# Block sums of the step-0 weights made from the first half step on, and copies of the original blocks issued by SyncE at later half steps

## The chip, the core and the metric

The kernel runs on one core of one Trainium2 chip. The metric is the device time of one execution in microseconds (us). A core has five engines that run side by side and meet at semaphores: TensorE (PE, matmul), VectorE (DVE), ScalarE (ACT), GpSimd (POOL) and SyncE (SP). Here SyncE and ScalarE issue the DMAs. Every engine takes its own instructions in program order, so an instruction that waits holds up all that stand behind it on the same engine.

## The reference

Two blocks follow each other on x (2 batches, 2048 rows, 512 features), all in float32:

```
mod = t @ Wm + bm                         # shifts, scales, gates from the condition
y   = y + gate_a * s5(ln(y) * (1 + scale_a) + shift_a)      # a linear recurrence over time
y_mod = (ln(y) * (1 + scale_c) + shift_c) * (1 + scale_ff) + shift_ff
y   = y + gate_ff * (gelu(y_mod @ W1 + b1) @ W2 + b2)       # 512 -> 2048 -> 512
h   = gamma * (ln(y) * ln_g + ln_b) + beta                  # gamma, beta from the condition
q, k, v = h @ Wqkv.T + bqkv               # 16 heads of 32
out = (softmax(q k^T) / sqrt(512)) v @ Wp.T + bp
h1  = out + y;  result = sln(h1) + h1
```

Only the first block and the q, k, v products matter for this change.

## The kernel before

The rows are cut into 8 chunks of 512. Up to about 1150 us the program goes through steps 0 to 7: step i does the feed-forward of chunk i beside the recurrence of chunk i + 1 and the q, k, v products of chunk i - 1. Attention follows.

**Seven products for eight.** From step 1 on, every product with w1, w2, wk, wq and wv is a two by two block product done with seven block products. For that each weight matrix is needed as seven blocks: three of its four original blocks (index 0, 3 and 4) and four sums or differences of blocks (1, 2, 5 and 6). They are made once, in step 0, and stored in DRAM: `w1d` (8 parts), `wkd` (2 parts for k, 2 for q), `wvd` (2 parts) and `w2d` (8 parts). From step 1 on `more` (line 866) streams them back through a ring of four tiles, `wring`. Its first three slots are those of the plain weights wk, wq and wv.

**Step 0 itself** (lines 1064 to 1076) still uses the plain weights. It runs over f = 0 to 15. For each f, `ff_first` (line 593) multiplies by one column block of w1 and ScalarE applies gelu to give `hid` (line 600); `ff_second` (line 604) multiplies by w2 for f - 1. After `ff_first` and after `ff_second` the program calls `run_due`, so there are 32 half steps, numbered h = 2f or 2f + 1; what the dictionary `due` lists for a half step is written into the program there, in order of the list. The order is fixed by hand.

What `due` held already (lines 1030 to 1048 and 1054 to 1058): `gate_of_feed_forward` at h = 2 and `rest_of_mod` at h = 3, both through `modulate` (line 235); `s5_gates` at 4; at 5 `rows_of_biases`, the norm of chunk 1 (`normalised`), its turn into features (`s5_blocks`: four VectorE transposes, line 498, then 16 DMAs on SyncE, line 503) and `s5_direct` (12 GpSimd operations); `s5_features` (ScalarE, line 479) at 10 to 13; `s5_in` (TensorE, line 531) and `s5_turn` (lines 541 and 543) at 13; `s5_scan` and a load of x at 14; `s5_out` (lines 578 to 582) at 18 to 21; at 22 three `more` on SyncE, then `ff_norm` and `by_blocks` (again transposes and 16 DMAs, this time `moved`); `ff_features` (ScalarE, line 479) from 26.

`modulate` lets TensorE make a product `pq`, ScalarE copy it to the tile `quarters` (line 251), and TensorE sum the quarters (line 240). The tile's slot is `hid0`, `hid1` or `hid2` by m modulo 3: GATE_F (m = 5) and GAMMA (m = 8) use `hid2`, BETA `hid0`. These slots have one buffer.

**The jobs.** There are 22: jobs 0 to 7 for w1 (`by_columns`), 8 and 9 for wk, 10 and 11 for wq, 12 and 13 for wv (`by_rows_v`), 14 to 21 for w2 (`by_rows_w2`). Job n runs on VectorE if n mod 3 is 2, otherwise on GpSimd. `combine` (line 795) makes two pairs of sums with two operations each (lines 801, 802 and 805, 806) and issues a SyncE DMA of 256 KB for each pair (line 807). The first pair's tile is in slot `hi` (two buffers) for GpSimd or `hid2` (one buffer) for VectorE; the second pair's is in `lo` (two buffers, both engines). For w1, wk, wq and wv the job also issues three copies of original blocks, 128 KB each, through `plain` (line 810), on ScalarE's queue. `w2_originals` (line 852) does so for w2 with three copies of 1 MB. The weights themselves come in by SyncE loads ahead of step 0; wk, wq and wv are the last (line 767).

Of the kernel before, what the change touches and what calls it, by code (L numbers as in the profile page):

```python
# [39 lines left out]
def tile_s5_block_then_sln_attention(  # L40
# [21 lines left out]
    nc = tc.nc  # L62
# [49 lines left out]
    HC = CH // 2  # L112
    w1d = dpool.tile([FH, P, 7, HC], F32, name="w1d")
    w2d = dpool.tile([7, P, FH, HC], F32, name="w2d")
# [167 lines left out]
    w2_sb = [hpool.tile([P, FH, D], F32, name=f"w2_{j}", tag=f"h{j}") for j in range(2)]  # L282
# [147 lines left out]
    def norm_steps(b, c):  # L430

        held = {}

        def row(t):
            if t == 0:
                held["mv"] = small.tile([P, TT, 2], F32, name="ln_mv", tag=f"ln_mv{TT}")
            ln_row(xt[b, c], t, held["mv"])

        def scale():
            held["mean"] = small.tile([P, TT], F32, name="mean")  # L440
            held["rstd"] = small.tile([P, TT], F32, name="rstd")
            ln_scale(held["mv"], TT, held["mean"], held["rstd"])

        def to(t):
            if t == 0:
                xns[b, c] = xnp.tile([P, TT, D], F32, name="xn", tag="xn")
            normalise(xns[b, c][:, t, :], xt[b, c][:, t, :], held["mean"], held["rstd"], t)

        return [(row, t) for t in range(TT)], [(scale,)], [(to, t) for t in range(TT)]
# [69 lines left out]
    def tag_of(b, c):  # L519
        return f"f{index[b, c] % 2}"  # L520
# [72 lines left out]
    def ff_first(b, c, f):  # L593
        ph = ps1.tile([P, CH], F32, name="ph")
        for k in range(KC):
            nc.tensor.matmul(
                ph, w1_sb[:, k, f * P : (f + 1) * P], fts[b, c][:, k, :], start=k == 0, stop=k == KC - 1
            )
        hids[f] = work1.tile([P, CH], F32, name="hid", tag=f"hid{f % 2}", bufs=1)
        nc.scalar.activation(  # L600
            in_time(hids[f], b, c), as_made(ph, b, c), AF.Gelu_apprx_tanh, bias=vec[:, V_B1 + f : V_B1 + f + 1], scale=1.0
        )

    def ff_second(b, c, f):
        if f == 0:
            pos[b, c] = ps1.tile([P, TT, D], F32, name="po", bufs=1)
        hid = hids.pop(f)
        for t in range(TT):
            nc.tensor.matmul(
                pos[b, c][:, t, :], hid[:, t * P : (t + 1) * P], w2_sb[f // FH][:, f % FH, :],  # L610
                start=f == 0, stop=f == FC - 1,
            )
# [182 lines left out]
    def combine(block, to, *shape, engine=nc.gpsimd):  # L795

        for at, tag in ((1, "hi"), (5, "lo")) if engine is nc.gpsimd else ((1, "hid2"), (5, "lo")):
            pair = work1.tile([P, 2, HC], F32, name="sums", tag=tag, bufs=1 if tag == "hid2" else 2)
            views = [pair[:, m, :].rearrange("p (k f) -> p k f", k=shape[0]) for m in range(2)]
            if at == 1:  # L800
                engine.tensor_tensor(views[1], block(1, 0), block(1, 1), ALU.add)
                engine.tensor_tensor(views[0], views[1], block(0, 0), ALU.subtract)
                s2 = views[0]
            else:
                engine.tensor_tensor(views[0], block(0, 0), block(1, 0), ALU.subtract)
                engine.tensor_tensor(views[1], block(0, 1), s2, ALU.subtract)
            nc.sync.dma_start(to(at, at + 2), pair)

    def plain(block, to, m, i, j):
        nc.scalar.dma_start(to(m, m + 1), block(i, j))  # L810

    ORIGINALS = ((0, 0, 0), (3, 0, 1), (4, 1, 1))

    def by_columns(w, half, p, dst, engine):

        def block(i, j):
            return w[:, 2 * j : 2 * j + 2, half * i + P * p : half * i + P * p + P]

        def to(m0, m1):
            if m1 - m0 == 1:  # L820
                return dst[:, m0, :].rearrange("p (k f) -> p k f", k=2)
            return dst[:, m0:m1, :]

        combine(block, to, 2, engine=engine)
        for m, i, j in ORIGINALS:
            plain(block, to, m, i, j)

    def by_rows_w2(q, engine):

# [8 lines left out]
    def by_rows_v(w, q, engine):  # L838

        def block(i, j):  # L840
            return w[:, 2 * j + q : 2 * j + q + 1, HC * i : HC * i + HC]

        def to(m0, m1):
            return wvd[:, m0:m1, q, :]

        combine(block, to, 1, engine=engine)
        for m, i, j in ORIGINALS:
            plain(block, to, m, i, j)

    def w2_originals():  # L850
        for m, i, j in ORIGINALS:
            nc.scalar.dma_start(w2d[m], w2_sb[j][:, :, HC * i : HC * i + HC])

    stream, slots, ready = [], ["wk", "wq", "wv", "w3"], []
    for i in range(1, len(order)):
# [10 lines left out]
    def more(engine=nc.scalar):  # L866

        n = begun[0]
        if n == total:
            return  # L870
        begun[0] += 1
        tag = slots[n % 4]
        src, size = stream[n]
        w = (strip if tag == "w3" else wlate).tile([P, FH * HC], F32, name="wring", tag=tag)
        engine.dma_start(w[:, :size], src)
        ready.append(w)
# [21 lines left out]
    def ff_sums(b, c, engine):  # L898
        parts_of["ff"] = sums_of(*quarters_of(fts[b, c], TT), engine, TT, "parts")
# [121 lines left out]
    for i, now in enumerate(order[:1]):  # L1021

        due = {(f, h): [] for f in range(FC + 1) for h in range(2)}
        ahead = order[i + 1]

        def quarters_from(f, what, chunk):
            for k in range(KC):
                due[f + k // 2, k % 2].append((what, *chunk, k))

        due[1, 0].append((gate_of_feed_forward,))  # L1030
        due[1, 1].append((rest_of_mod,))
        due[2, 0].append((s5_gates, start[0]))
        due[2, 1].append((rows_of_biases,))
        due[2, 1].append((normalised, *ahead))
        due[2, 1].append((s5_blocks, *ahead))
        due[2, 1].append((s5_direct, *ahead))
        quarters_from(5, s5_features, ahead)
        due[6, 1].append((s5_in, *ahead))
        due[6, 1].append((s5_turn, *ahead))
        due[7, 0].append((s5_scan, *ahead))  # L1040
        quarters_from(9, s5_out, ahead)
        due[11, 0].append((ff_norm, *ahead))
        due[11, 0].append((by_blocks, *ahead, tag_of(*ahead)))
        quarters_from(13, ff_features, ahead)
        due[7, 0].append((load_x, *order[i + 2]))
        jobs = [(by_columns, w1_sb, FH * P, p, w1d[p]) for p in range(FH)]
        jobs += [(by_columns, w, HC, p, wkd[2 * n + p]) for n, w in enumerate((wk, wq)) for p in range(2)]
        jobs += [(by_rows_v, wv, q) for q in range(2)]
        jobs += [(by_rows_w2, q) for q in range(FH)]
        for n, job in enumerate(jobs):  # L1050
            h = 6 + 4 * n // 5
            due[h // 2, h % 2].append((*job, nc.vector if n % 3 == 2 else nc.gpsimd))
        due[9, 0].append((w2_originals,))
        for n in range(3):
            due[11, 0].insert(0, (more, nc.sync))

        later[order[2]] = norm_steps(*order[2])
        due[12, 1] += later[order[2]][0]

        def run_due(at):  # L1060
            for what, *args in due[at]:
                what(*args)

        for f in range(FC):
            ff_first(*now, f)
            run_due((f, 0))
            if f == FC - 1:
                first.close()
                strip = early.enter_context(tc.tile_pool(name="strip", bufs=1, side="right"))
                ff_sums(*ahead, nc.vector)  # L1070
                more()
            if f:
                ff_second(*now, f - 1)
            run_due((f, 1))
        ff_second(*now, FC - 1)
        ff_out(*now)
        first_banks.close()
        psq = early.enter_context(tc.tile_pool(name="psq", bufs=6, space=PSUM, side="right"))

    for i, now in enumerate(order):  # L1080
# [20 lines left out]
        if ahead:  # L1101
            rows, scale, to = later.pop(ahead)
# [57 lines left out]
        if ahead:  # L1160
            rows, scale, to = norm_steps(*ahead)
# [528 lines left out]
    keeps, m = [], 0  # L1690
# [16 lines left out]
    due = {}  # L1707
# [21 lines left out]
    for b in range(NB):  # L1729
        for c in range(NQ):  # L1730
            j = NP * (blocks.index((b, NPAIR - 1, c)) + 1) + 1
            if (b, c) == (LB, LC):
                most, rest = slice(0, NH - 4), slice(NH - 4, NH - 2)
                j = NP * (N - 1)
# [55 lines left out]
    def block_at(j):  # L1790
        n, i = divmod(j, NP)
        return (n, i) if 0 <= n < N else (None, i)

    for j in range(FIRST, NP * N + 2):
# [16 lines left out]
        n, i = block_at(j + AHEAD)  # L1811
# [26 lines left out]
        n, i = block_at(j + 1)  # L1838
# [4 lines left out]
        n, i = block_at(j - 1)  # L1843
# [59 lines left out]
```

## Time and profile before

| what | value |
|---|---|
| time, median of 3 runs | 3296.51 us (3296.01 to 3299.68) |
| time of the profiled execution | 3303.55 us |
| its span, first to last instruction | 3300.4 us |
| mean granted TensorE clock | 0.988 |
| step 0 on TensorE | 66.5 to 218.3 us |
| TensorE busy, 120 to 140 us | 15.57 of 20 us, clock 0.83 |
| TensorE busy, 200 to 220 us | 14.91 of 20 us, clock 0.91 |
| TensorE busy, 140 to 200 us | 60.0 of 60 us |

A line of the trace's order of time gives the start in us, the duration in us, the engine, the line of the kernel, the operation, the tile written and the tiles read, the shape, how many instructions were merged, and in brackets how long the engine was idle before and what ended that. An engine name with a q (SPq, ACTq) is its sequencer issuing DMAs; this is not counted as busy time. In a group line of the page the last part is the same idle time for the whole group.

### The profile page before, as it was taken

Reading aid. Unit: us, or ns where it says so; the run is one execution under the profiler, and the core shown is the slowest. Engines: PE = TensorE matmul, PEld = TensorE weight load, DVE = VectorE, ACT = ScalarE, POOL = GpSimd, SP = SyncE. Lnnn points to the kernel's source line nnn. Section 1 sums busy time; section 2 is a strip of 40 time slices with the busy share of each in tenths; the row PEclk is TensorE's granted clock in tenths of the full one; section 3 lists DMA queues with packets and bytes.
Section 4 is the critical chain, followed back from the end, with each engine's and each line's share of the span. In section 5 each row is a group of like instructions: output and inputs, shape, how many; then the busy total and the mean of one; then the engine's idle time right before and its main releaser. Section 6 shows DMA issues by size and latency. Waiting matters only on the chain.

```text
span 3300.4 us, 38742 instructions
## 1 busy us (share of the span) xinstructions
PE 3178.3 (96%) x12900; PEld 1768.0 (54%) x12900; DVE 2406.2 (73%) x3226; ACT 2015.7 (61%) x2393; POOL 2385.6 (72%) x1438
## 2 busy tenths in 40 slices
PE   7999999999999998999999999999999999999996
PEld 4458888888888884344444444444444444443432
DVE  5455565656565434888888888888888888888884
ACT  2111213121221212899999999999888898898862
POOL 1646454554546331799989999998899899999986
PEclk9999999999999998999999999999999999999998
DMA  8556757667575664332322223133233333333233
GB/s 306 186 173 185 234 177 229 196 195 246 157 241 174 221 205 151 80 87 50 76 70 56 70 65 74 50 78 80 70 80 92 85 77 93 79 75 87 66 102 97
DMA packets 298012, 422.18 MB, mean 128 GB/s; under 512 B 98712, under 2 KB 195224, under 8 KB 286678
## 3 DMA queue, kind: packets, MB, share of 16 engines
q1 hardware_dynamic: 254758, 269.63, 30.2%
q10 hardware_dynamic: 43056, 150.09, 14.0%
q8 instruction: 102, 1.67, 0.2%
q14 instruction: 96, 0.79, 0.1%
HBM read 309.38 MB, written 87.94 MB: 120 GB/s over the span
## 4 chain that ended last, share of the span: by engine, by line
PE 25%; ACT 16%; DVE 13%; issue 3%; DMA 3%; POOL 1%; SPq 1%; ACTq 0%; DVEq 0%; POOLq 0%
PE o L1399 11%; PE s L1330 8%; DVE run L1346 7%; ACT x L1341 7%; ACT x L1389 5%; ACT pT L1389 4%; PE py L1482 3%; DVE pT L1384 3%; DVE run L1350 2%; PE pt_run L1358 1%; DMA by<-invd 1%; POOL x L1378 1%; PE pk L657 1%; DMA ks<-kd 1%; DVE st L1499 0%
## 5 line engine op out<-in xcount | busy, mean ns | idle before, releaser
L1378 POOL TENSOR_TENSOR x<-x,shift 128x1024 f32<-128x1024 f32 x704 | 1653.2, 2389 | 132.2 <-DMA shift<-flat 113.7
L1330 PE MATMUL s<-qs,ks 128*128 128x512 f32 x2688 | 823.1, 427 | 51.8 <-DVE run L1346 32.3
L1341 ACT COPY x<-s 128x1024 f32<-128x1024 f32 x704 | 691.8, 1010 | 148.6 <-PE s L1330 132.1
L1346 DVE TENSOR_TENSOR run<-s,run 128x1024 f32<-128x1024 f32 x576 | 705.1, 1224 | 80.7 <-ACT x L1341 36.8
L1389 ACT ACTIVATE x<-x 128x1024 f32<-128x1024 f32 x704 | 738.0, 1058 | 20.6 <-POOL x L1378 20.0
L1399 PE MATMUL o<-x,v 128*64 128x512 f32 x2816 | 718.1, 612 | 0.0
L1330 PEld LDWEIGHTS s<-qs,ks 128*128 128x128 f32 x2688 | 444.7, 189 | 466.1 <-DVE run L1346 161.0
L1384 DVE TENSOR_TENSOR pT<-s,shift 128x1024 f32<-128x1024 f32 x320 | 388.8, 1215 | 50.5 <-PE s L1330 50.5
L1350 DVE TENSOR_TENSOR run<-s,run 128x1024 f32<-128x1024 f32 x320 | 389.2, 1216 | 10.1 <-PE s L1330 9.7
L1389 ACT ACTIVATE pT<-pT 128x1024 f32<-128x1024 f32 x320 | 339.4, 1061 | 74.7 <-DVE pT L1384 74.6
L1399 PE MATMUL o<-pT,v 128*64 128x512 f32 x1280 | 329.2, 593 | 6.6 <-ACT pT L1389 6.6
L1399 PEld LDWEIGHTS o<-x,v 128*64 128x64 f32 x2816 | 157.1, 135 | 309.5 <-issue 251.3
L920 PE MATMUL pp<-parts,wring 128*128 128x256 f32 x1344 | 318.0, 379 | 0.0
L973 PE MATMUL pp<-wring,h 128*128 128x256 f32 x1344 | 293.3, 379 | 0.0
L973 PEld LDWEIGHTS pp<-wring,h 128*128 128x128 f32 x1344 | 255.4, 190 | 39.8 <-issue 5.7
L920 PEld LDWEIGHTS pp<-parts,wring 128*128 128x128 f32 x1344 | 255.9, 190 | 35.0
L920 PE MATMUL pp<-fT,wring 128*128 128x256 f32 x1008 | 249.5, 381 | 7.6 <-ACT hid L619 2.8
L920 PEld LDWEIGHTS pp<-fT,wring 128*128 128x128 f32 x1008 | 191.1, 190 | 39.2 <-DVE zb L957 3.8
L1399 PEld LDWEIGHTS o<-pT,v 128*64 128x64 f32 x1280 | 91.3, 137 | 191.3 <-issue 142.3
L1096 POOL TENSOR_TENSOR h<-h 128x256 f32<-128x256 f32 x56 | 42.7, 763 | 191.1 <-ACT h L1094 191.1
L1346 DVE TENSOR_TENSOR run<-s,x 128x1024 f32<-128x1024 f32 x64 | 78.4, 1225 | 114.2 <-ACT x L1341 114.2
L479 ACT ACTIVATE fT<-moved,s_shift,s_scale 128x512 f32<-128x512 f32 x28 | 20.5, 802 | 200.2 <-DMA moved<-fT 170.5
(379 smaller groups left out, 3111.6 us busy)
## 6 DMA issues: line engine op xcount, KB each, us to landing
wring<-w2d ACTq DMA_DIRECT2D x49, 1024.0 KB
wring<-w1d ACTq DMA_DIRECT2D x53, 896.0 KB
ks<-kd SPq DMA_DIRECT2D x128, 256.0 KB
shift<-flat SPq DMA_DIRECT2D x64, 512.0 KB
qs<-qd SPq DMA_DIRECT2D x496, 64.0 KB
wring<-wkd ACTq DMA_DIRECT2D x28, 896.0 KB
moved<-fT SPq DMA_DIRECT2D x168, 64.0 KB
x<-in_x SPq DMA_DIRECT2D x8, 1024.0 KB
```

Of the source, the lines that this page charges most:

```text
L920: nc.tensor.matmul(to, w[:, m, k, :], moving, start=start and k == 0, stop=stop and k == 1, skip_group_check=True,)
L973: nc.tensor.matmul(out[:, t * HC : t * HC + HC], x(m, q, t), w[:, q, :], start=start and q == 0 and t == 0, stop=stop and q == depth - 1 a ...
L1096: nc.gpsimd.tensor_tensor(h1[:, p, HC:], h1[:, p, HC:], h1[:, p, :HC], ALU.subtract)
L1330: nc.tensor.matmul(s[:, e, :], kst[pair_of[n], e][:, kt * P : (kt + 1) * P], qst[n][:, e, :], start=True, stop=True,)
L1341: nc.scalar.copy(x, s)
L1346: nc.vector.tensor_tensor(runs[n], s, kept[n, 0] if kt == 1 else runs[n], ALU.max)
L1350: nc.vector.tensor_tensor(runs[n], raw_scores(n, kt), runs[n], ALU.max)
L1378: nc.gpsimd.tensor_tensor(x, x, shifts[n], ALU.add)
L1384: nc.vector.tensor_tensor(x, s, shifts[n], ALU.add)
L1389: nc.scalar.activation(x, x, AF.Exp)
L1399: nc.tensor.matmul(outs[n][64 * e : 64 * e + 64, :], v[:, kt, e : e + 2, :], x[:, e, :], start=first, stop=final,)
L1482: nc.tensor.matmul(py, o4[:, g, :], wp[:, g, :], start=g == 0, stop=g == NG - 1)
```

## The change

The sums and the copies of originals become separate entries of `due`. A job called with an engine only makes sums and stores them; the same job called with `None` only copies the originals. The copies go from ScalarE's queue to SyncE's.

Jobs 0 to 13 (w1, wk, wq, wv) make their sums at half steps 0 to 4, at the front of each half step's list (of several at one half step the later job stands first); before, they were at 6 to 16, at the end of the lists. Jobs 14 to 21 (w2) make theirs at 6 to 13 instead of 17 to 22. The copies of jobs 0 to 13 are at 5 to 10, at the end of the lists, and those of w2 at 12 instead of 18.

```diff
     def plain(block, to, m, i, j):
-        nc.scalar.dma_start(to(m, m + 1), block(i, j))
+        nc.sync.dma_start(to(m, m + 1), block(i, j))
...
-        combine(block, to, 2, engine=engine)
-        for m, i, j in ORIGINALS:
-            plain(block, to, m, i, j)
+        if engine is None:
+            for m, i, j in ORIGINALS:
+                plain(block, to, m, i, j)
+        else:
+            combine(block, to, 2, engine=engine)
...
     def w2_originals():
         for m, i, j in ORIGINALS:
-            nc.scalar.dma_start(w2d[m], w2_sb[j][:, :, HC * i : HC * i + HC])
+            nc.sync.dma_start(w2d[m], w2_sb[j][:, :, HC * i : HC * i + HC])
...
         for n, job in enumerate(jobs):
-            h = 6 + 4 * n // 5
-            due[h // 2, h % 2].append((*job, nc.vector if n % 3 == 2 else nc.gpsimd))
-        due[9, 0].append((w2_originals,))
+            h = 5 * n // 14 if n < 14 else n - 8
+            engine = nc.vector if n % 3 == 2 else nc.gpsimd
+            due[h // 2, h % 2].insert(0, (*job, engine))
+        for n, job in enumerate(jobs[:14]):
+            h = 5 + 3 * n // 7
+            due[h // 2, h % 2].append((*job, None))
+        due[6, 0].append((w2_originals,))
```

`by_rows_v` changes as `by_columns` does.

More of the change, by code (lines that the diff above doesn't have):

```diff
@@ L844, in to @@
             return wvd[:, m0:m1, q, :]
-        combine(block, to, 1, engine=engine)
-        for m, i, j in ORIGINALS:
-            plain(block, to, m, i, j)
+        if engine is None:
+            for m, i, j in ORIGINALS:
+                plain(block, to, m, i, j)
+        else:
+            combine(block, to, 1, engine=engine)
     def w2_originals():
         for m, i, j in ORIGINALS:
-            nc.scalar.dma_start(w2d[m], w2_sb[j][:, :, HC * i : HC * i + HC])
+            nc.sync.dma_start(w2d[m], w2_sb[j][:, :, HC * i : HC * i + HC])
     stream, slots, ready = [], ["wk", "wq", "wv", "w3"], []
```

## The prediction

> **What bounds the kernel now.** I read the page first, for the shares; then the tensor engine's order of time through step 0, for its gaps; then the order of time of ScalarE, VectorE, GpSimd and SyncE around each gap. The page has TensorE busy for 96% of the span, and in its forty slices only the first falls well below the rest:
>
> ```profile
> PE 3178.3 (96%) x12900; PEld 1768.0 (54%) x12900; DVE 2406.2 (73%) x3226; ACT 2015.7 (61%) x2393; POOL 2385.6 (72%) x1438
> PE   7999999999999998999999999999999999999996
> ```
>
> So an edit inside step 0 (66 to 218 us) counts only through gaps of TensorE that it closes or opens; what it closes there is kept, since from 224 us on TensorE goes from matmul to matmul (20.0 us busy in most 20 us windows up to 420). Step 0 has two places that this edit can reach. TensorE's order of time (start, duration, idle before it):
>
> ```profile
> 125.94 1.88 PE L531 MATMUL pu<-fT,bT_re 128*128 128x512 f32 x4
> 130.17 1.13 PE L531 MATMUL pu<-fT,bT_re 128*128 128x512 f32 x2 [2.35 <-ACT fT L479]
> 133.37 2.07 PE L531 MATMUL pu<-fT,bT_re 128*128 128x512 f32 x2 [2.07 <-ACT fT L479]
> 135.24 5.34 PE L531 MATMUL pu<-fT,bT_im 128*128 128x512 f32 x8
> 140.42 3.60 PE L596 MATMUL ph<-fT,w_sb 128*128 128x512 f32 x8
> ...
> 202.48 3.60 PE L596 MATMUL ph<-fT,w_sb 128*128 128x512 f32 x8
> 209.50 8.83 PE L609 MATMUL po<-w,hid 128*128 128x512 f32 x16 [3.42 <-ACT hid L600]
> ```
>
> Eight full-speed matmuls take 3.43 us from start to start (140.42 to 143.85). **Place a**: the 16 of s5_in take 14.48 us (125.94 to 140.42) where 6.87 would do: 7.6 us lost. Both gaps wait for ScalarE's features, and between 132.0 and 138.8 the granted clock was 0.50. **Place b**: 3.59 us of wait, and 8.83 where 7.03 is usual (the clock was 0.51 from 210.5 to 213.9): 5.4 us lost.
>
> Why a? ScalarE's order of time; ACTq lines are DMAs that it issues:
>
> ```profile
> 118.71 6.00 ACTq L810 DMA_DIRECT2D w1d<-w_sb  x5
> 124.76 0.81 ACT L479 ACTIVATE fT<-fT,mod,u_scale 128x512 f32<-128x512 f32 x1 [7.47 <-DMA w1d<-w_sb]
> 126.99 1.65 ACTq L810 DMA_DIRECT2D w1d<-w_sb  x3
> ...
> 129.47 2.98 ACTq L810 DMA_DIRECT2D wkd<-wk  x3
> 132.51 0.81 ACT L479 ACTIVATE fT<-fT,mod,u_scale 128x512 f32<-128x512 f32 x1 [2.39 <-DMA wkd<-wk]
> ```
>
> The features' inputs had landed at 112.6 (the trace's landing records). ScalarE was held by copies it had to issue. A copy starts only once the eighth DMA before it in the program has landed: those issued at 118.71, 120.80, 122.67 and 123.80 follow landings at 118.69, 120.78, 122.64 and 123.77, mostly of sums that SyncE had issued after waiting for GpSimd. Why b? ScalarE waits 14.23 us for `moved` (207.36), which follows VectorE's second norm; that is late because gate products of s5_out wait behind block sums (L805 at 166.63 waited 5.25 us for a DMA, so pa of 158.4 is read at 167.31).
>
> **What is removed.** All 45 copies leave ScalarE. In order: hid 5, two features, hid 6, two features, each 0.7 to 0.8 us, so all four are done before TensorE needs them: **a, -7.6 us**. The block sums of w2 end by half step 13, before s5_out at 18. Then gate product, add, statistics, norm (3.82, still beside GpSimd's adds), turn (2.48) and 16 moves (194.62 to 207.10, 12.5 us) follow the last s5_out by some 25 us, and TensorE's work up to that place takes 31 us (175.02 to 206.08): **b, -5.4 us**. Cover there is 6 us; without it b returns.
>
> **What is added early.** The jobs of half steps 0 to 4 stand ahead of everything else there. The one to fear is slot hid2 (one buffer): VectorE's jobs 2, 5, 8, 11 use it, and so do the `quarters` that ScalarE writes in modulate for GATE_F (m = 5) and GAMMA (m = 8). In the new program GATE_F's quarters stand behind job 8 and must wait until its first pair of sums has landed in DRAM. The same reuse shows before:
>
> ```profile
> 98.43 1.22 DVE L801 TENSOR_TENSOR sums<-w_sb 128x256 f32<-128x256 f32 x1
> 99.68 1.37 DVE L802 TENSOR_TENSOR sums<-sums,w_sb 128x256 f32<-128x256 f32 x1
> 117.34 0.97 DVE L805 TENSOR_TENSOR sums<-w_sb 128x256 f32<-128x256 f32 x1 [16.29 <-POOL sums L805]
> ...
> 120.86 0.99 DVE L801 TENSOR_TENSOR sums<-w_sb 128x256 f32<-128x256 f32 x1 [1.69 <-issue]
> ```
>
> The pair made at 98 to 101 was issued only at 118.46 (SyncE had two GpSimd jobs before it), landed at 120.78, and the next VectorE job wrote hid2 at 120.86. The second half (L805) waited likewise for slot `lo`, which has two buffers for both engines.
>
> The chain in the new kernel, with these prices: two GpSimd sums 1.45 us (0.72 each), an issue 0.35, issue to landing 2.03 (113.83 to 115.87), 0.68 between landings. wv lands at 70.84 on the same queue, so job 2's pairs land at 71.5 and 72.2, job 1's at 72.9 and 73.6. GpSimd then fills `lo` for job 0 (73.7, landed 75.9), job 4's `lo` (77.4), job 3's hi (78.9) and `lo` (80.4). Job 5's first pair lands at 76.5, so VectorE makes job 8's by 78, but SyncE issues it behind job 3's, at 80.8: landed near 83.2. Quarters to 83.9, and the sums of L240 start at 84 to 85 where they started at 77.30: 7.2 us later. TensorE is idle for 4 to 6 us before, so the clock halves: the cases above and the 0.50 from 60.3 to 70.5 cost 1.5 to 3.4 us each, say 2.3. **Early: +9.5 us.** Bounds: 4.8, if the pairs needn't queue behind the loads (3.3 earlier, clock 1.5), to 11.4. GAMMA's quarters want job 11's pair, landed near 90; TensorE gets there at 93, so this hides. GpSimd's first sums (56.4 to 61) run beside VectorE's first norm and cost it about 1.6 us (L125, 0.17 alone, took 0.65 beside GpSimd at 185.44); the 84 us is reached anyway, so that is free here. SyncE issues the 28 early pairs by 107, and the turn of the next chunk, slowed by GpSimd's sums, ends near 110.5 (98.5 + 9.5 + 2.5), so the moves aren't delayed by the pairs.
>
> **What SyncE gets.** 16 moves from 110.5 (0.645 each) to 120.8, landed by 122.9; TensorE wants them near 126. Behind them come 42 copies and w2's sums. Five unhindered copies of wq were issued 0.54 us apart (144.14 to 146.36); a pair of w2 costs 0.75. Thirty copies and ten pairs stand up to job 18: 120.8 + 16.2 + 7.5 = 144.5 for the last issue at best, 147 with the bubbles between; job 20 on VectorE needs job 18's `lo` (149.5), job 21 on GpSimd job 19's (153.5), and **s5_turn stands behind both**. From 150: four products 2.4, add 0.6, two scans 2.33 (43.31), GpSimd's four at 1.27: states ready near 160.4. TensorE wants them at 159.5 (s5_in's end 142.4, plus 17.1 as from 140.42 to 157.59): **+0.9 us**. Bounds: 0 with copies at 0.41 (ACTq's closest issues) up to 10 with copies at 0.84 (ACTq's ten L810 lines sum to 35.2 us for 42); 0.54 is the row that waited for nothing. w2's three copies and the ring's loads follow, by 180, ahead of the second `moved`: no price.
>
> **Sum**: 9.5 + 0.9 - 7.6 - 5.4 = -2.6 us. Span 3300.4 becomes 3297.8, the profiled 3303.55 about 3301; that execution lies 7 us above the median, so I take the difference: 3296.5 - 2.6 = **3294**.
>
> The Trainium skill, "TensorE: Matmul & The Clock Gate" (What's actually happening), halves the clock only after an idle window of about 3.4 us. Here two gaps of 2.35 and 2.07 us were enough, so the measurement decides. By the page alone, place a would be worth an estimated 4.4 us instead of 7.6, and the sum +0.6.
>
> The Trainium skill, "DMA: Bandwidth & Descriptors" (Issuing engines are not separate DMA queues), speaks against the move: a second issuing engine saves only issue time. That would make the copies' new queue worth nothing by itself; the rows above say that issue on ScalarE, with its waits, is what place a pays for.
>
> **Rivals.** A: the early wait isn't there, because the pairs land sooner than GATE_F's quarters come. Then only VectorE's 1.6 us remains: 1.6 - 13.0 = -11.4, **3285**. For it: pairs are ready by 66 to 74. Against: the single hid2 slot and SyncE's order, as at 118.46. B: SyncE's copies take 0.84 us apart, as on ScalarE. Thirty are 9 us later; s5_turn follows, TensorE waits some 9 us before s5_out and a halved clock adds 1.7: -2.6 + 10.5 = +7.9, **3304**. It decides from about 0.60 us a copy. For it: 512-byte pieces, one queue. Against: the 0.54 rows. C: the change doesn't free the features, since moves landing late hold them, and a stays: -2.6 + 7.6 = +5.0, **3301.5**.
>
> **Numbers.** Forecast 0.62 (3288 to 3299), A 0.13, B 0.18, C 0.07. A measurement of this kernel can tell about 0.2% (6.6 us) from no change. Faster by more: A and 0.07 of the forecast's low end, 0.20. Slower by more: B without its milder 0.02, 0.16. Within: 0.64. The range, 3288 to 3305, leaves out A and B's worst, under 0.2.
>
> **What would show it.** L240 of GATE_F near 84 with an idle time before it that names ScalarE's quarters; no gap in L531; no ACTq copies before 200; the L600/L609 gap near 209 gone; s5_out within 2 us of L596's end. I am wrong if L240 stays under 80, or if L578 first waits over 4 us.

## The result and the profile after

The changed kernel takes 3307.07 us (median of 20 runs) where the kernel before takes 3301.16 beside it (20 runs): ratio 1.0017, 95% interval 1.0010 to 1.0024. By the interval it is 3 to 8 us slower; the forecast was 2.6 us faster. In a second comparison it took 3304.70 against 3300.60, ratio 1.0013 (1.0005 to 1.0022). The medians of the kernel before in these comparisons, 3300 to 3301, lie above the 3296.5 that the prediction started from.

TensorE's order of time in the changed kernel, at the places that the prediction named (start, duration, idle before it and what ended that):

```profile
73.25 1.07 PE L247 MATMUL pq<-wm,cond_q 128*32 128x512 f32 x8
84.10 1.87 PE L240 MATMUL pg<-four,quarters 128*128 128x2 f32 x8 [9.78 <-ACT quarters L251]
...
136.46 3.60 PE L531 MATMUL pu<-fT,bT_re 128*128 128x512 f32 x8
139.89 3.60 PE L531 MATMUL pu<-fT,bT_im 128*128 128x512 f32 x8
143.33 3.60 PE L596 MATMUL ph<-fT,w_sb 128*128 128x512 f32 x8
...
163.98 1.86 PE L578 MATMUL pa<-c_re,m 128*128 128x512 f32 x2 [3.33 <-DVE m L557]
165.63 1.91 PE L579 MATMUL pa<-c_im,m 128*128 128x512 f32 x2
...
210.39 3.60 PE L596 MATMUL ph<-fT,w_sb 128*128 128x512 f32 x8
213.82 7.03 PE L609 MATMUL po<-w,hid 128*128 128x512 f32 x16
```

Both places that lost time before are closed: s5_in runs from 136.46 to 143.33 without a gap (place a), and the last two ff_second follow at once and take 7.03 us (place b). Two new gaps stand against them: 9.78 us before L240 and 3.33 us before the first s5_out.

ScalarE says what the first gap is. In its order of time the copy of quarters stood still for 9.36 us, until a DMA of sums of wk, job 8, had landed (at 83.32, by the trace's landing records):

```profile
73.42 0.69 ACT L600 ACTIVATE hid<-ph,vec 128x512 f32<-128x512 f32 x1 [2.81 <-PE ph L596]
83.46 0.59 ACT L251 COPY quarters<-pq 128x512 f32<-128x512 f32 x1 [9.36 <-DMA wkd<-sums]
```

The table of the two queues on the page shows that the change did what it says: 8.65 MB (42 copies of 128 KB, three of 1 MB) went from ScalarE's queue q10 (150.09 MB before) to SyncE's q1 (269.63 before).

```profile
q1 hardware_dynamic: 268534, 278.28, 31.4%
q10 hardware_dynamic: 29280, 141.44, 13.0%
```

To follow the time through step 0, this table gives when TensorE starts six pieces of work, in us, from the order of time of each trace (the experiments are told below):

| kernel | L240 (GATE_F) | ff_first, f = 2 | ff_first behind s5_in | first s5_out | ff_second, f = 14 | step 1 |
|---|---|---|---|---|---|---|
| before, first trace | 77.30 | 87.95 | 140.42 | 157.59 | 209.50 | 221.13 |
| before, second | 76.21 | 86.86 | 139.49 | 156.66 | 208.68 | 220.31 |
| before, third | 74.10 | 84.76 | 136.11 | 153.28 | 205.42 | 216.77 |
| changed, first | 84.10 | 98.47 | 143.33 | 163.98 | 213.82 | 223.65 |
| changed, second | 83.89 | 96.95 | 141.81 | 163.18 | 213.79 | 223.62 |
| quarters in own slot | 79.62 | 92.52 | 137.37 | 161.07 | 211.19 | 221.02 |
| copies behind the scan | 84.25 | 98.45 | 143.31 | 160.47 | 208.54 | 218.37 |
| both | 77.76 | 92.26 | 137.11 | 154.28 | 202.35 | 212.17 |
| before, copies on SyncE | 76.43 | 87.09 | 131.94 | 149.11 | 204.29 | 217.08 |
| both, all jobs behind | 77.38 | 88.21 | 133.36 | 150.53 | 203.53 | 215.16 |
| changed, copies on ScalarE | 84.18 | 97.30 | 166.79 | 183.96 | 232.02 | 241.85 |
| both, two half steps behind | 79.92 | 90.58 | 135.43 | 153.19 | 201.33 | 211.16 |

Changed against before, first traces: +6.8 at L240, +10.5 at f = 2, +2.9 behind s5_in, +6.4 at s5_out (+8.2 at the next s5_out, 170.90 against 162.74), +4.3 at f = 14, +2.5 at step 1.

### The profile page after: what moved, and what is told of

Read it like the earlier page. It is cut to its first block, busy times and chain, and to the rows that moved or that the text cites. A ratio compares the mean times of both kernels' runs of the same rounds, so it can differ in the third digit from the quotient of the medians.

```text
span 3304.7 us, 38756 instructions
## 1 busy us (share of the span) xinstructions
PE 3174.8 (96%) x12900; PEld 1766.5 (53%) x12900; DVE 2410.7 (73%) x3226; ACT 2015.2 (61%) x2393; POOL 2385.4 (72%) x1438
## 4 chain that ended last, share of the span: by engine, by line
PE 22%; ACT 16%; DVE 13%; DMA 4%; POOL 3%; issue 3%; SPq 1%; ACTq 0%; DVEq 0%; POOLq 0%
PE o L1407 9%; PE s L1338 7%; DVE run L1354 7%; ACT x L1349 7%; ACT x L1397 5%; ACT pT L1397 4%; POOL x L1386 3%; DVE pT L1392 3%; PE py L1490 2%; DVE run L1358 2%; DMA by<-invd 1%; PE pt_run L1366 1%; PE pk L657 1%; DMA shift<-flat 1%; PE pv L669 0%
```

## The experiments

**1. The quarters in a slot of their own.** Changed kernel, with:

```diff
-            quarters = work1.tile([P, D], F32, name="quarters", tag=f"hid{m % 3}", bufs=1)
+            quarters = work1.tile([P, D], F32, name="quarters", tag="gated" if m in (GATE_F, GAMMA) else f"hid{m % 3}", bufs=2 if m in (GATE_F, GAMMA) else 1)
```

> The changed kernel, but the quarters of GATE_F and GAMMA are written to slot gated, which no block sum uses. Theory 1 (the early loss is the wait for slot hid2): the sums of L240 start at 77 to 78 us instead of 84.10 and the gap of 9.78 us goes. But the turn of the next chunk and SyncE's copies then come only some 7.5 us earlier, since the early pairs still hold SyncE until about 104, while TensorE comes 10 us earlier: the states of the recurrence are ready near 156, TensorE wants them near 150, and the wait before s5_out grows from 3.3 to about 6.5 us. Total about 7 us below the changed kernel, 1 to 5 us below the kernel before. Rival (the early loss is GpSimd's sums beside the first norm, or the load of the queue): L240 stays near 84 and the time does not move.

Measured: 3301.66 us against 3300.60, ratio 1.0004 (0.9995 to 1.0013); 3 us below the changed kernel on the same chip. TensorE's order of time:

```profile
79.62 1.05 PE L240 MATMUL pg<-four,quarters 128*128 128x2 f32 x8 [0.76 <-ACT quarters L251]
81.79 1.13 PE L177 MATMUL pt_ar<-ident,gate_b 128*128 128x128 f32 x8 [1.11 <-DVE gate_b L777]
...
161.07 2.04 PE L578 MATMUL pa<-c_re,m 128*128 128x512 f32 x2 [6.37 <-DVE m L557]
```

The gap before L240 falls from 9.78 to 0.76 us: slot hid2 was its cause. The wait before s5_out grows to 6.37, as expected: TensorE ends s5_in 6.0 us earlier (137.37 instead of 143.33), and the recurrence has its last state only 2.9 us earlier (160.92 instead of 163.83). So this loss and the next overlap; whoever removes the first alone gets about a third of it. The size was off: 3 us below the changed kernel where about 7 were expected, and 1 us above the kernel before, not 1 to 5 below (the interval reaches from 2 us below to 4 above).

**2. The copies behind the scan.** Changed kernel, with:

```diff
-            h = 5 + 3 * n // 7
+            h = 14 + 3 * n // 7
...
-        due[6, 0].append((w2_originals,))
+        due[10, 0].append((w2_originals,))
```

> The changed kernel, but the copies of the original blocks of w1, k, q and v stand at half steps 14 to 19 and those of w2 at 20, behind s5_turn and s5_scan. Theory 1 (the wait before s5_out comes from w2's sums, whose buffers are freed late because SyncE issues the copies in between): the early wait at L240 stays near 84, s5_turn starts right behind s5_in near 143, the 3.33 us gap at L578 and the halved clock behind it go, and the time is 5 us below the changed kernel, about as the kernel before or up to 3 us below. Rival (the recurrence's own operations on VectorE and GpSimd hinder each other and are too slow): the gap at L578 stays above 2 us.

Measured: 3300.70 us against 3300.60, ratio 0.9998 (0.9989 to 1.0007); 4 us below the changed kernel on the same chip. TensorE reaches s5_out without a wait:

```profile
157.04 3.60 PE L596 MATMUL ph<-fT,w_sb 128*128 128x512 f32 x8
160.47 1.02 PE L578 MATMUL pa<-c_re,m 128*128 128x512 f32 x2
161.33 1.02 PE L579 MATMUL pa<-c_im,m 128*128 128x512 f32 x2
```

The copies between w2's sums on SyncE were the cause of the second gap. VectorE's order of time in the same run answers part of the rival too:

```profile
143.51 0.69 DVE L541 TENSOR_TENSOR m<-pu,t_im 128x512 f32<-128x512 f32 x1 [2.14 <-PE pu L531]
...
145.43 3.35 DVE L551 TENSOR_TENSOR_SCAN m<-decay,last,m 128x512 f32<-128x512 f32 x2
148.71 1.69 DVE L553 TENSOR_TENSOR m<-m,t_re 128x512 f32<-128x512 f32 x1
150.32 1.75 DVE L555 TENSOR_TENSOR m<-m,t_im 128x512 f32<-128x512 f32 x1
152.10 1.64 DVE L557 TENSOR_TENSOR m<-m,m 128x512 f32<-128x512 f32 x1
```

No block sum runs here any more, and still the scans take 3.35 us (2.33 at the start of the kernel, where VectorE does all of it alone) and L553 to L557 1.64 to 1.75 each (0.68 there). GpSimd's own four operations of the recurrence run at those times. That the two engines hinder each other is read from these rows; no run takes GpSimd's half away at this place. Here it costs nothing: the states are ready at 153.74, over 6 us before TensorE wants them at 160.47.

**3. Both edits.**

> Both edits: the quarters in slot gated, and the copies behind the scan. Theory 1: no gap of TensorE above 1 us from 66 to 217 us, all of what the two places of the kernel before lost (13 us) is gained: 11 to 13 us below the kernel before, 17 to 19 below the changed kernel. Rival: the gains do not add up, because with TensorE 10 us earlier the turn of the next chunk, behind the early pairs on SyncE, comes too late for the features; then a gap at L531 names ScalarE's features.

Measured: 3294.22 us against 3300.60, ratio 0.9980 (0.9971 to 0.9989): 6.4 us faster than the kernel before, where 11 to 13 were expected. TensorE's order of time has one gap left between 66 and 206 us that is longer than 1 us:

```profile
81.71 2.05 PE L177 MATMUL pt_ar<-ident,gate_b 128*128 128x128 f32 x8 [2.90 <-DVE gate_b L777]
```

So a part of the early loss remains by another way: VectorE makes gate_b2 only behind job 8's sums, which stand ahead of it and wait for a landing. VectorE's order of time:

```profile
79.55 0.55 DVE L805 TENSOR_TENSOR sums<-wk 128x256 f32<-128x256 f32 x1 [0.99 <-DMA w1d<-sums]
...
81.07 0.49 DVE L777 TENSOR_TENSOR gate_b<-mod,vec 128x8 f32<-128x8 f32 x1
```

The clock record has one more halved window behind it (81.4 to 84.8 us), and ff_first of f = 2 starts 4.3 us later than in the first trace of before. The expected gap-free step was wrong in this. Another part stands ahead of 66 us: before L750, TensorE waits for VectorE's first norm, 5.9 us with the old order of jobs and some 7.2 us with the new one (8.1 in experiment 7). The prediction priced this hindrance by GpSimd's first sums at 1.6 us; it is free only as long as L240 is held until 84.

**4. The kernel before and the changed kernel again**, for more traces. Neither has an edit.

> The changed kernel again, for the part of its loss that step 0 of the first trace does not show (2.5 us of 5.9 between the medians). If that part is a property of the kernel, the trace again shows a growing distance behind step 0, at the same places; if it is the clock's windows falling differently from run to run, the distance at 260 us is again 1 to 4 us and wanders elsewhere.

> The kernel before again, for a second trace. All four other kernels' medians lie 2.5 to 4 us further above the kernel before than their traces lie above its first trace at 240 us. If the first trace of before is an unlucky one, TensorE reaches the same instruction there some 3 us earlier here, with the halved clock after the gaps of place a or b shorter than in the first trace, and the two gaps themselves (about 4.4 and 3.4 us) unchanged. If the first trace is typical, it comes within 1 us of it.

> As the second trace of the kernel before: whether the halved clock behind places a and b costs the same each time (7.6 and 5.4 us in all in the first trace), or differs by up to 3 us with where the clock's windows fall.

Measured: the changed kernel reaches step 1 at 223.62, against 223.65 the first time. The kernel before reaches it at 220.31 and 216.77, against 221.13. So the first trace of before was the slowest of three in step 0; the mean is 219.4, and the changed kernel stands 4.2 us above it. By the measure set beforehand the second trace (0.8 us earlier) calls the first typical; only the third (4.4 us earlier) does not, so this mean rests on few executions. TensorE's order of time in the third shows where it differs:

```profile
74.10 1.05 PE L240 MATMUL pg<-four,quarters 128*128 128x2 f32 x8 [0.70 <-ACT quarters L251]
...
127.25 1.13 PE L531 MATMUL pu<-fT,bT_re 128*128 128x512 f32 x2 [2.62 <-ACT fT L479]
130.28 2.07 PE L531 MATMUL pu<-fT,bT_re 128*128 128x512 f32 x2 [1.91 <-ACT fT L479]
...
205.42 8.55 PE L609 MATMUL po<-w,hid 128*128 128x512 f32 x16 [3.79 <-ACT hid L600]
216.77 1.13 PE L920 MATMUL pp<-fT,wring 128*128 128x256 f32 x4 [2.80 <-ACT hid L619]
```

The gaps are nearly the same (2.62 and 1.91 at place a, 3.79 at place b), but L240 came at 74.10 (77.30 and 76.21 in the others), and the clock was halved for 3.4 us behind place a instead of 6.8. Of the 4.4 us to the first trace, 2.0 lie in the very first ff_first (7.13 us for its 16 matmuls instead of 9.09), 1.1 in place a and 1.2 in an earlier start of step 0. In all four traces that keep the wait on slot hid2, L240 starts between 83.89 and 84.25, though TensorE is done with the work before it anywhere between 74 and 79: there it hangs on the landing of the loads and of the sums queued behind them, and what TensorE gained before is lost in the wait. The part of the loss beyond step 0 wanders: at the end of the span the second trace of the changed kernel lies 0.8 us below the first of before, the first 4.3 above.

**5. The queue alone.** Kernel before, with the copies on SyncE at their old half steps (the two lines of the diff with `nc.sync`).

> The kernel before with one part of the change: its copies go over SyncE's queue, at the old half steps. Theory (place a was ScalarE's issuing of copies): both gaps at L531 go, since ScalarE issues nothing in step 0, which gives up to 7 us; but SyncE issues each job's copies between the pairs of sums, so buffers of the sums are freed later, s5_turn and the second norm come later than before, and place b stays or grows (3 to 10 us), with a wait before s5_out possible. Total between 4 us faster and 5 us slower. Rival (the features are held by something else): the gaps at L531 stay.

Measured: 3298.78 us against 3300.79, ratio 0.9994 (0.9985 to 1.0003). TensorE's order of time has no gap at L531, and these two later:

```profile
125.08 3.60 PE L531 MATMUL pu<-fT,bT_re 128*128 128x512 f32 x8
128.51 3.60 PE L531 MATMUL pu<-fT,bT_im 128*128 128x512 f32 x8
131.94 3.60 PE L596 MATMUL ph<-fT,w_sb 128*128 128x512 f32 x8
...
160.95 1.13 PE L578 MATMUL pa<-c_re,m 128*128 128x512 f32 x2 [1.37 <-DVE gated L581]
...
204.29 9.99 PE L609 MATMUL po<-w,hid 128*128 128x512 f32 x16 [5.31 <-ACT hid L600]
```

Place a is gone by the change of queue alone: -0.9 us before s5_in and -8.5 behind it (131.94 against 140.42) make 7.6. Place b is larger, 5.31 us of wait instead of 3.42: w2's sums still stand beside s5_out and the second norm. So the queue closes a. That the earlier sums close b follows from all traces together: b is open in the three of before and here, where w2's sums are late, and closed in those with early sums, with copies early or late and on either queue (experiment 7 is the exception, told there).

**6. The queue undone.** Changed kernel, with the copies on ScalarE at their new half steps.

> The changed kernel with one part undone: the copies go over ScalarE's queue again, at their new half steps. Theory (place a is ScalarE held by copies that stand ahead of the features): with the sums done early the copies wait for less, but 42 copies at 0.54 us are 23 us of issue on ScalarE from about 119 on, and the copies of jobs 12 and 13 stand between the first and the second feature, so the second to fourth feature come near 142 instead of 127 to 135 and a gap of some 5 us opens again at L531. SyncE then issues w2's sums without copies between, so the gap at L578 (3.3 us) goes. Total within 4 us of the changed kernel. Rival (only the time of the sums mattered, the queue of the copies nothing): no gap at L531, none at L578, 5 us faster than the changed kernel.

Measured: 3325.18 us against 3300.14, ratio 1.0074 (1.0060 to 1.0088): 25 us slower than before. ScalarE's order of time:

```profile
124.72 2.33 ACTq L810 DMA_DIRECT2D w1d<-w_sb  x3
127.32 7.11 ACTq L810 DMA_DIRECT2D wkd<-wk  x6
134.47 5.29 ACTq L810 DMA_DIRECT2D wkd<-wq  x6
139.86 0.69 ACT L600 ACTIVATE hid<-ph,vec 128x512 f32<-128x512 f32 x1 [14.54 <-DMA wkd<-wq]
...
147.83 10.96 ACTq L856 DMA_DIRECT2D w2d<-w  x1
158.83 0.81 ACT L479 ACTIVATE fT<-fT,mod,u_scale 128x512 f32<-128x512 f32 x1 [11.07 <-issue]
```

TensorE waits 8.09 us for this hid (L609 at 140.60) and 10.76 us for this feature (L531 at 159.70). The direction was right, the size was not (I had expected it within 4 us of the changed kernel): I had counted the issue of the copies, and not gelu held by them nor a copy of 1 MB that waits. The gap at L578 is gone, as expected. The copies at these half steps need the new queue.

**7. Both edits, and all early jobs behind their half step's list** instead of at its front (`append` for `insert(0, ...)`).

> As the kernel with both edits (quarters in slot gated, copies behind the scan), but each job of sums stands at the end of its half step's list instead of the front. There, VectorE had to finish job 8's sums, which wait for a landing, before it could make gate_b2: TensorE waited 2.90 us before L177, and the clock halved. Theory: this wait falls to about 0.55 us, the halved window behind it goes, and the time is 2 to 5 us below that kernel, 9 to 11 below the kernel before. Rival (the halved clock follows from the gaps before 66 us alone): the gap goes but the time moves by 2 us at most; or the norm of chunk 1, behind job 11 on VectorE now, comes late and a gap opens at L531.

Measured: 3297.99 us against 3300.79, ratio 0.9991 (0.9982 to 1.0000): 2.8 us below the kernel before, where 9 to 11 were expected, and a smaller gain than in experiment 3, though the two intervals overlap. The wait for gate_b2 is gone (0.73 us), but place b is back (3.38 us before L609, for ScalarE's hid behind `moved`). SyncE's order of time:

```profile
122.00 26.78 SPq L807 DMA_DIRECT2D w2d<-sums  x16
...
174.16 2.81 SPq L856 DMA_DIRECT2D w2d<-w  x3
177.02 5.45 SPq L879 DMA_DIRECT2D wring<-w1d  x3
182.51 17.29 SPq L503 DMA_DIRECT2D moved<-fT  x16
```

In experiment 3 w2's pairs end at 139.0 and the ring's loads are issued at 168. Here job 21 stands behind s5_turn, so its pairs hold SyncE until 148.8, everything behind them moves by 9 us, and 2.7 MB of ring loads are queued just ahead of the moves, which take 17.29 us instead of 10.34. The landing records show how: by the rule of the eighth DMA that the prediction read from them, the sixth to eighth move each wait for a ring load; they are issued at 188.31, 190.48 and 193.23, and the three loads land at 188.30, 190.46 and 193.21.

**8. Both edits, and only the jobs of half steps 2 and 3 behind.**

```diff
-            due[h // 2, h % 2].insert(0, (*job, engine))
+            due[h // 2, h % 2].insert(len(due[h // 2, h % 2]) if h in (2, 3) else 0, (*job, engine))
```

> The kernel with both edits (quarters in slot gated, copies behind the scan), and of the early jobs only those of half steps 2 and 3 behind the gate and modulation steps; job 21 stays ahead of s5_turn, so SyncE isn't held by it before the copies as in the variant with all jobs behind, where place b came back. Theory: the wait of 2.90 us before L177 goes (0.55 stays) with half a clock window, place b stays closed as in the kernel with both edits (moves issued near 181): 2 to 4 us below that kernel, 8 to 11 us below the kernel before. Rival: VectorE's jobs 8 and 11, now behind GpSimd's on SyncE, hold the norm of chunk 1, the chain on SyncE shifts, and b or a gap at L531 takes the gain back.

Measured: 3292.05 us against 3300.14, ratio 0.9974 (0.9965 to 0.9983): 8.1 us faster than the kernel before (5.6 to 11.6 by the interval). It is the lowest median of all, but not clear of experiment 3, whose interval overlaps and which ran on another chip. The wait before L177 is 0.55 us and place b stays closed, as expected. These are all the gaps in TensorE's order of time from L240 to the start of step 1:

```profile
79.92 1.05 PE L240 MATMUL pg<-four,quarters 128*128 128x2 f32 x8 [0.76 <-ACT quarters L251]
81.53 1.13 PE L177 MATMUL pt_ar<-ident,gate_b 128*128 128x128 f32 x8 [0.55 <-DVE gate_b L777]
...
153.19 1.10 PE L578 MATMUL pa<-c_re,m 128*128 128x512 f32 x2 [0.43 <-DVE m L557]
...
211.16 1.13 PE L924 MATMUL pp<-fT,wring 128*128 128x256 f32 x4 [2.80 <-ACT hid L619]
```

## Why the prediction was wrong, point by point

**Place a, -7.6 us: right.** +10.5 before s5_in and +2.9 behind it make 7.6; experiment 5 has the same from the queue alone. The 7.6 contain 4.4 of waits and 3.2 of halved clock. The second part changes from execution to execution: in the third trace of before the place costs 6.5.

**Place b, -5.4 us: right.** +7.9 at the start of the last ff_first (210.39 against 202.48), +2.5 at step 1. Experiment 5, which keeps w2's sums late, keeps b; experiment 7 brings it back although most sums are early, so the cover that the prediction named is needed.

**Early, +9.5 us: the mechanism right, the size 1 us short.** L240 at "84 to 85" came at 84.10, and job 8's pair, "landed near 83.2", landed at 83.32. L240 came 6.8 us later than before, not 7.2, and the clock cost 3.7 instead of 2.3: TensorE's granted clock was 0.60 from 84.1 to 94.5 us. Experiment 1 shows slot hid2 as the cause.

**s5_turn, +0.9 us: this step failed in its size.** It cost 5.0: +2.9 ahead of it, +6.4 at the first s5_out, +7.9 by the end of the four. The start of the chain was nearly right: job 20's second pair could be written at 150.28 ("149.5"). The chain itself was not. VectorE's order of time in the changed kernel:

```profile
150.28 0.42 DVE L805 TENSOR_TENSOR sums<-w 128x256 f32<-128x256 f32 x1 [5.58 <-DMA w2d<-sums]
...
151.50 0.68 DVE L541 TENSOR_TENSOR m<-pu,t_re 128x512 f32<-128x512 f32 x1
...
154.92 1.63 DVE L551 TENSOR_TENSOR_SCAN m<-decay,last,m 128x512 f32<-128x512 f32 x1
157.65 2.27 DVE L551 TENSOR_TENSOR_SCAN m<-decay,last,m 128x512 f32<-128x512 f32 x1 [1.09 <-POOL m L543]
159.84 0.66 DVE L553 TENSOR_TENSOR m<-m,t_re 128x512 f32<-128x512 f32 x1
160.42 1.75 DVE L555 TENSOR_TENSOR m<-m,t_im 128x512 f32<-128x512 f32 x1
162.20 1.63 DVE L557 TENSOR_TENSOR m<-m,m 128x512 f32<-128x512 f32 x1
```

I took two scans at 2.33 us, from 43.31, where no GpSimd operation runs. The trace of before had the same step at 142.54, beside GpSimd's half and its block sums, and that row should have been used:

```profile
43.31 2.33 DVE L551 TENSOR_TENSOR_SCAN m<-decay,m 128x512 f32<-128x512 f32 x2
...
142.54 3.77 DVE L551 TENSOR_TENSOR_SCAN m<-decay,last,m 128x512 f32<-128x512 f32 x2
```

In the changed kernel the two scans take 3.90 us, and between them VectorE waits 1.09 us for GpSimd's L543, which stood behind job 21's sums until 155.43 and then took 2.18 us. From the first product to the last state the chain took 12.3 us, not 10.4, and began at 151.5, not 150. So the states came 3.4 us later than I had them (163.8), TensorE wanted them 1.0 later (160.5), and it waited 3.33 us (4.05 in the second trace). The halved clock behind that, which the +0.9 did not contain at all, cost 1.5 to 1.8 more (the first s5_out and its ff_second take 170.90 - 163.98 = 6.92 us, where 5.15 are usual). Experiment 2 shows that the whole wait goes when SyncE issues no copies between w2's sums. The rival B had this place and a price of about 10; its own reason, copies at 0.84 us, was wrong: they were issued 0.54 apart, as forecast.

**The sum.** With +10.5 and +5.0 it is 15.5 - 13.0 = +2.5, the distance at step 1 of the first traces. **From trace to median** a second step failed, as far as three traces show: "I take the difference" assumes that the profiled execution's step 0 is that of the median. It was the slowest of three, and its 3303.55 us lie 2.4 above the median of 20 runs. What the change pins to the loads (L240 at 84) does not get faster when a run is faster before it, so a loss priced against a slow execution is too small. This gives 1.7 us more at step 1. Together 4.2, against 5.9 and 4.1 between the medians; what remains is within the intervals, and its cause stays open.

**The time itself.** Some 13 us lie between 3294 and 3307.07: 4.7 are the starting point (3296.5 from three runs, 3301.16 from 20), 5.1 the terms (-2.6 became +2.5), 3.4 the way from trace to median. The starting point was chance; the rest is the two steps above and the 1 us of the early term.

Two slips in the prediction carry nothing: the lower bound of the early term, from its own numbers, is 7.2 - 3.3 + 1.5 = 5.4, not 4.8; and the last of the page's forty slices (6) is as low as the first (7).

**Issuing from a second engine.** The Trainium skill, "DMA: Bandwidth & Descriptors" (Issuing engines are not separate DMA queues), was cited in the prediction for the rule that a second issuing engine saves only issue time. Experiments 5 and 6 show what that leaves out: the engine that issues also waits, in order, and gelu and features stood behind it. With the copies on ScalarE the new order takes 25 us more than the kernel before; with them on SyncE it takes 4.1 to 5.9 more.

## What to carry to other kernels

When work is moved ahead of a step, list every buffer slot it shares with what now stands behind it: one single-buffered slot turned an early sum into a 9.78 us wait of TensorE, through a third engine. Price a chain of two engines by rows in which both run. Add the halved clock to a wait of TensorE: behind every one of 3.3 us or more in step 0 of the twelve traces it was there. Losses by different waits in a row do not add: removing one let the next one grow from 3.33 to 6.37 us. Either edit alone left the time at that of the kernel before; both together made the change a gain (ratio 0.9980, and 0.9974 with two half steps of jobs placed so that neither VectorE nor SyncE was held).

## What the runs showed of the hardware

The same gap of 2.80 us before step 1 was followed by a halved clock (3.4 us) in the first two traces of before, and by full clock in its third and in the changed kernel; over all twelve traces it was halved in four. The halved stretches of a trace stand on one grid: in the first of before they begin at 60.24, 131.92, 210.43 and 220.67 us, whole multiples of 3.413 us apart, and the grid lies differently in each execution. The Trainium skill, "TensorE: Matmul & The Clock Gate" (What's actually happening), says that the clock's window runs freely and isn't reset by the kernel; these traces agree, and differ from its rule that a whole idle window of about 3.4 us is needed (the waits of place a are 1.91 to 2.62 us). So one kernel reaches step 1 at times 4.4 us apart (216.77 to 221.13) with nearly the same gaps, 3.1 of them by the halved clock, and a change of a few us needs more than one trace.
